# Three layers of an image network: waits of each tile's own place, a bias on ScalarE, and another order of seven products

## The chip, the core and the metric

The kernel runs on one core of a Trainium2 chip. The metric is device time in microseconds (us) of one execution, taken as the median over several runs. One further execution was recorded by the profiler. Engines are named as in the profile: PE (TensorE, matmuls), DVE (VectorE), ACT (ScalarE), POOL (GpSimd), SP (the queue that issues most transfers). "P1" to "P7" are the seven products of Strassen's method.

## The reference

The input x has two images of 512 channels and 32 x 32 positions, in float32. Four layers follow each other; the output of one is the input of the next.

```python
# layer 0: deformable attention with a learned position bias, then an MLP
attn = softmax(q @ k + cpb_mlp(positions));  x = x + out_w @ (attn @ v) + out_b
x = x + mlp_w2 @ gelu(mlp_w1 @ bn2(x) + mlp_b1) + mlp_b2
# layer 1: linear attention
Q, K, V = wq @ x + bq, wk @ x + bk, wv @ x + bv
Q, K = Q / norm(Q), K / norm(K)                       # over the 64 channels
tailor = 1 / (n + Q^T @ (K.sum(-1) + eps))
x = x + gamma * (V.sum(-1) + Q^T @ (K @ V^T)) * tailor
# layers 2 and 3: group norm, attention with 8 heads of 64, projection, residual
qkv = qkv_w @ group_norm(x) + qkv_b
a = softmax(q^T @ k * scale) @ v                      # per head
x = x + proj_w @ a + proj_b
```

## The kernel before

x stays in SBUF for the whole kernel: `self.xs[b][t]`, for image b and a block t of 128 channels, 1024 positions wide. The class `Net` has one method per stage. In time they follow each other: layer 0 with its position bias and attention (to about 2045 us), its MLP `mlp0` (2046 to 2431), `layer1` (2431 to 2500), and `attention` twice, for k = 2 (2500 to 2943) and k = 3 (2943 to the end).

Every tile comes from a pool that a stage opens and closes (`Net.pool`, L68). A pool opened later lies on bytes that closed pools left. By default a tile in such a pool waits until every user of all those pools has finished. The framework can also make it wait only for the users of the bytes under this very tile (for PSUM, of its bank).

Where a block stands under `manual_schedule`, the engines named there execute in the order of the program text. Elsewhere a scheduler orders the instructions of an engine.

**MLP.** `mlp0` runs eight slabs of two times seven products (`m_0P` to `m_7P`, L729). Weights are prepared by left sums (L707 to L710) on POOL.

**Layer 1.** `l1qk` (L894) makes queries and keys of both images. `l1t` (L909) transposes x, block by block of positions; even blocks are copied to SBUF by ACT (L913), odd ones by DVE (L915). POOL squares, DVE reduces, ACT takes the root, DVE divides. Then the written order begins: `keys_sum` (kb), `divisors`, `keys_x` (m1), `keys_column`, `turned` (transposed queries, qt), `matrix` (m and the tile mat), `result` (w, L1002). For image 0 DVE adds w to x; for image 1 ACT copies it to ws (L1011) and POOL adds (L1012). Between them stand the statistics and the first normalized block of layer 2 (`channel_means`, `group_means`, `norm_first`: L1283 to L1324). The PSUM pools are ps_t (three buffers, transposes), ps_m and ps (three buffers, everything else).

**Heads (k = 2, 3).** `queries_keys_values` makes q, k and v with seven products each (qk20P and so on, L1152), with left sums of the weights on POOL. `heads_bounded` then goes through 16 units, each an image b, a pair p of heads, and a half h of the queries (512 positions). A unit has eight steps n. In the written order, `score` of a step (L1366, then the exponential L1370 on ACT) stands two steps ahead of its `value` (L1395). The exponentials are summed on POOL (`some`, L1375, L1377) and on DVE (`sum`, L1380 to L1384). Four steps into the next unit comes `divide`: matmuls sum over partitions (d, L1412), ACT copies one half, DVE adds the other, takes the reciprocal (L1418), multiplies (L1420) and adds the bias of v (L1421). The scheduler places ACT's work; PE, DVE and POOL keep the written order.

In the second half of the units, `sums` for the projection are spread over POOL, three per unit and later two (L1431, and left sums). The last subtracts, `late`, run on DVE after the last divide.

PSUM places have names, and `place(spot, name)` gives the next tile in one: "a", "b", "even", "odd".

**Projection.** `project(b)` makes seven products for image b. Each has two halves of the output, and DVE, ACT or POOL adds each half to those blocks of x that need it. `add(eng, p, i, what)` adds to block i of half p, from PSUM or from a tile; u (and u3) are sums over products that several blocks share. `store(p, i)` in layer 3 writes a finished block to memory from SP. Before, the products come in this order, with the sums u and u3 in SBUF:

```python
for which, spot in zip(("P1", "P3", "P2", "P6", "P7", "P5", "P4"), at):
```

With k = 2 the second projection also carries the start of layer 3's normalization: `channel_means(3, 0, t)` for four channel blocks, `group_means` (matmul gm3, L1290, then dv, L1293 to L1295, and a second matmul L1297, sc and off L1298 to L1310), and `norm_first` (xn300, L1324).

Of the kernel before, what the change touches and what calls it, by code (L numbers as in the profile page):

```python
# [11 lines left out]
F32 = mybir.dt.float32  # L12
# [6 lines left out]
P = 128  # L19
# [35 lines left out]
class Net:  # L55
# [808 lines left out]
    def layer1(self, w, bias):  # L864
# [3 lines left out]
        with ExitStack() as ctx:  # L868
            pool = self.pool(ctx, "l1")
            small = self.pool(ctx, "l1s", 3)  # L870
            last = self.pool(ctx, "l1w", 4)
            ps_t = self.pool(ctx, "l1_ps_t", 3, psum=True)
            ps_m = self.pool(ctx, "l1_ps_m", 1, psum=True)
# [11 lines left out]
            for b in range(B):  # L885
                qk.append(pool.tile([P, NB, 2, DH], F32, tag=f"qk{b}", name=f"qk{b}"))
                xT.append(pool.tile([P, NB, C], F32, tag=f"xT{b}", name=f"xT{b}"))
                for half in range(2):
                    qk_ps = ps.tile([P, 4, P], F32, tag="ps", name=f"l1qk{b}{half}")
                    for i in range(4):  # L890
                        n = 4 * half + i
                        for t in range(CT):
                            xt = self.xs[b][t][:, n * P : (n + 1) * P]
                            nc.tensor.matmul(  # L894
                                qk_ps[:, i, :], lhsT=xt, rhs=w[:, t, C:640], start=(t == 0), stop=(t == CT - 1)
                            )
                    nc.vector.tensor_tensor(
                        qk[b][:, 4 * half : 4 * half + 4, :, :].rearrange("p n a d -> p n (a d)"),
                        qk_ps,
                        bias[:, C:640].unsqueeze(1).to_broadcast([P, 4, P]),  # L900
                        ALU.add,
                    )
            for b in range(B):
                sq = pool.tile([P, NB, 2, DH], F32, tag=f"sq{b}", name=f"sq{b}")
                nc.gpsimd.tensor_tensor(sq, qk[b], qk[b], ALU.mult)
                for n in range(NB):
                    tr = ps_t.tile([P, C], F32, tag="t", name=f"l1t{b}{n}")
                    for t in range(CT):
                        nc.tensor.transpose(  # L909
                            tr[:, t * P : (t + 1) * P], self.xs[b][t][:, n * P : (n + 1) * P], self.ident  # L910
                        )
                    if n % 2 == 0:
                        nc.scalar.copy(xT[b][:, n, :], tr)  # L913
                    else:
                        nc.vector.tensor_copy(xT[b][:, n, :], tr)  # L915
# [66 lines left out]

            def turned(b):
                for h in range(2):
                    tr = ps_t.tile([P, HF], F32, tag="t", name=f"qt{b}{h}")
                    for n in range(4):
                        nc.tensor.transpose(tr[:, n * P : (n + 1) * P], qn[b][:, 4 * h + n, :], self.ident)
                    qa = pool.tile([DH + 1, HF], F32, tag=f"qa{b}{h}", name=f"qa{b}{h}")
                    act.copy(qa, tr[0 : DH + 1, :])
                    q_at.append(qa)  # L990

            def matrix(b):
# [24 lines left out]
            with self.tc.manual_schedule(engines=engines):  # L1017
# [5 lines left out]
                keys_column(0)  # L1023
                turned(0)
                matrix(0)
                keys_sum(1)

# [246 lines left out]

    def channel_means(self, k, b, t):
        nc, small = self.nc, self.norm
        if t == 0:
# [54 lines left out]
    def heads_bounded(self, k, ones, data, proj, out):  # L1332
# [7 lines left out]
        with ExitStack() as ctx:  # L1340
# [66 lines left out]
            def divide(unit):  # L1407
# [12 lines left out]
                nc.vector.tensor_tensor(res, res, t, ALU.mult)  # L1420
                nc.vector.tensor_scalar(res, res, self.col(f"vb{k}", p), None, ALU.add)  # L1421

# [4 lines left out]
            left = [proj[:, i] for i in range(4)] + [more[:, i] for i in range(3)]  # L1427
            right, sums, late = [], [], []

            def subtract(eng, to, x, y):  # L1430
                return lambda: eng.tensor_tensor(to, x, y, ALU.subtract)  # L1431

            for b in range(B):
# [8 lines left out]
                if b == 1:  # L1442
                    sums += self.left_steps(nc.gpsimd, proj, more)
                    sums += [subtract(nc.gpsimd, t1[c], r[1][c], r[0][c]) for c in range(2)]
                for c in range(2):
                    eng, to = (nc.vector, late) if b == c == 1 else (nc.gpsimd, sums)
                    if b == 0:
                        to.append(subtract(eng, t1[c], r[1][c], r[0][c]))
                    to.append(subtract(eng, t2[c], r[3][c], t1[c]))
                    to.append(subtract(eng, t3[c], r[3][c], r[1][c]))  # L1450
                    to.append(subtract(eng, t4[c], r[2][c], t2[c]))

            def project(b):
# [10 lines left out]
                def store(p, i):  # L1464
                    o = 2 * (i // 2) + p
                    cut = slice((i % 2) * HF, (i % 2 + 1) * HF)
                    if out is not None:
                        nc.sync.dma_start(out[b, o][:, cut], self.xs[b][o][:, cut])

                at = ("a", "b", "even", "a", "b", "even", "a") if b == 0 else ("odd", "even", "b", "odd", "even", "a", "b")  # L1470
                for which, spot in zip(("P1", "P3", "P2", "P6", "P7", "P5", "P4"), at):
                    a, ri = SEVEN[which]
                    if which == "P1":
                        us = ap2.tile([P, 2, HF], F32, tag="sum", name=f"pu{k}{b}")
                    elif which == "P7":
                        u3s = ap2.tile([P, 2, HF], F32, tag="sum", name=f"pv{k}{b}")
                    acc = place(spot, f"pb{k}{b}{which}")
# [289 lines left out]
```

## Time and profile before

| | us |
|---|---|
| median of three runs | 3387.63 (3387.11 to 3388.1) |
| the profiled execution | 3386.91 |
| its span, first to last instruction | 3385.1 |
| last matmul ends, from the span's start | 3377.07 |
| mean granted clock of TensorE | 0.999 |

Times in the text are microseconds from the span's start in the profiled execution. A group's line shows line, engine, operation, output and inputs with their shapes and the number of instructions; then its busy time, the mean of one in nanoseconds, and the idle time of the engine just ahead of them with what ended most of it. A waits line shows the waiting group, what it waited for, the total, how often, and the longest. A timeline line shows start, duration, engine, line, operation and tiles, and in square brackets the idle time ahead of it.

Busy time in microseconds by stage, in the same profile:

| stretch | PE | DVE | ACT | POOL |
|---|---|---|---|---|
| 2431 to 2500, layer 1 | 64.75 | 36.87 | 14.57 | 20.51 |
| 2627 to 2886, heads of layer 2 | 254.79 | 209.09 | 152.23 | 149.97 |
| 2886 to 2942, projection of layer 2 | 52.15 | 42.02 | 5.82 | 17.40 |
| 3070 to 3326, heads of layer 3 | 252.96 | 206.23 | 149.20 | 148.06 |
| 3326 to 3385, projection of layer 3 and end | 51.06 | 36.80 | 3.70 | 19.10 |

### The profile page before, as it was taken

To read this page: it belongs to the slowest core of one execution; us is meant where nothing else is said; L and a number is where in the kernel's file an instruction comes from. 1 tells how busy PE (TensorE), PEld (TensorE's weight loads), DVE (VectorE), ACT (ScalarE), POOL (GpSimd) and SP (SyncE) were. 2 spreads that over 40 slices of the span, in tenths; PEclk is the share of its full clock that TensorE was granted. 3 is DMA by queue.
4 is the path that set the end of the run, shared out by engine and by line. 5 is a ranking of instruction groups with operands and counts; after the bars stand their busy time and mean duration, and the time that the engine had idled before them with its cause. 6 is when DMAs were issued, how large, how long until landed. Compare 5 with 4: busy or idle time off the path is not lost.

```text
span 3385.1 us, 60157 instructions
## 1 busy us (share of the span) xinstructions
PE 3335.1 (99%) x25224; PEld 1241.3 (37%) x25224; DVE 2377.3 (70%) x2544; ACT 2040.8 (60%) x2152; POOL 2169.6 (64%) x1643
## 2 busy tenths in 40 slices
PE   7999999999999999999999999999999999999999
PEld 2333333333333333333333334444555433355433
DVE  6777777777766677777766664575466689765897
ACT  6887887887886688887887761111121566213662
POOL 4877877878877677878878873432324357444474
PEclk9999999999999999999999999999999999999999
DMA  6877877877877577877787861111000100000001
GB/s 164 160 148 156 159 156 149 165 155 156 161 155 144 118 158 147 165 155 156 161 171 159 161 158 64 50 37 38 0 1 2 37 2 1 14 0 13 1 1 51
DMA packets 102384, 342.66 MB, mean 101 GB/s; under 512 B 12624, under 2 KB 14288, under 8 KB 99024
## 3 DMA queue, kind: packets, MB, share of 16 engines
q0 software_dynamic: 73296, 266.90, 40.4%
q1 hardware_dynamic: 27792, 69.68, 7.2%
q8 instruction: 203, 3.33, 0.4%
q10 hardware_dynamic: 1008, 2.06, 0.2%
q14 instruction: 85, 0.70, 0.1%
HBM read 67.27 MB, written 4.46 MB: 21 GB/s over the span
## 4 chain that ended last, share of the span: by engine, by line
PE 90%; DVE 6%; POOL 2%; ACT 1%; issue 1%; DMA 0%; ACTq 0%; DVEq 0%; POOLq 0%
PE hp L559 51%; PE s L1366 4%; PE o L1395 4%; PE sim L591 3%; PE qk20P L1152 1%; PE qk30P L1152 1%; PE m_0P L729 1%; PE m_6P L729 1%; PE m_4P L729 1%; PE m_2P L729 1%; PE m_1P L729 1%; PE qk31P L1152 1%; PE qk21P L1152 1%; PE m_5P L729 1%; PE m_3P L729 1%; PE m_7P L729 1%
## 5 line engine op out<-in xcount | busy, mean ns | idle before, releaser
L559 PE MATMUL hp<-h,w 128*32 128x512 f32 x16384 | 1799.3, 593 | 3.0 <-DVE h L528 2.0
L528 DVE CUSTOM_DVE_ANT_1 h<-tx,bank 128x1024 f32<-128x1024 f32 x1024 | 1180.8, 1216 | 308.6 <-PE hp L559 236.8
L564 ACT ACTIVATE h<-hp,magb 128x1024 f32<-128x1024 f32 x1024 | 1120.7, 1111 | 378.0 <-PE hp L559 370.2
L559 PEld LDWEIGHTS hp<-h,w 128*32 128x32 f32 x16384 | 527.8, 110 | 1204.3 <-issue 1148.3
L551 POOL DMA_DIRECT2D h<-h x509 | 451.6, 1022 | 385.2 <-ACT h L570 323.3
L577 POOL TENSOR_TENSOR h<-h,h 128x1024 f32<-128x1024 f32 x255 | 610.0, 2392 | 21.3
L575 POOL TENSOR_SCALAR h<-h,flip 128x1024 f32<-128x1024 f32 x256 | 447.0, 1746 | 0.9 <-ACT h L564 0.9
L1370 ACT ACTIVATE e<-s 128x1024 f32<-128x1024 f32 x256 | 261.7, 1024 | 159.8 <-PE s L1366 159.1
L566 ACT ACTIVATE h<-h,flip 128x1024 f32<-128x1024 f32 x256 | 291.4, 1138 | 0.0
L1395 PE MATMUL o<-e,v 64*64 64x512 f32 x2048 | 267.7, 589 | 0.8 <-ACT e L1370 0.8
L1366 PE MATMUL s<-q,k 64*64 64x512 f32 x2048 | 267.9, 589 | 0.0
L1375 POOL TENSOR_TENSOR some<-e,e 128x1024 f32<-128x1024 f32 x32 | 75.5, 2360 | 172.6 <-DVE sum L1384 139.2
L1377 POOL TENSOR_TENSOR some<-some,e 128x1024 f32<-128x1024 f32 x64 | 167.0, 2609 | 23.7 <-ACT e L1370 20.1
L568 POOL TENSOR_SCALAR h<-h,flip 128x1024 f32<-128x1024 f32 x128 | 143.0, 1117 | 51.6 <-ACT h L564 50.7
L570 ACT ACTIVATE h<-h,flip 128x1024 f32<-128x1024 f32 x128 | 145.6, 1138 | 0.0
L591 PE MATMUL sim<-h,ends 128*32 128x512 f32 x1024 | 135.3, 592 | 0.1
L1395 PEld LDWEIGHTS o<-e,v 64*64 64x64 f32 x2048 | 83.3, 133 | 137.4 <-issue 132.0
L1366 PEld LDWEIGHTS s<-q,k 64*64 64x64 f32 x2048 | 83.2, 133 | 136.1 <-issue 123.5
L707 POOL TENSOR_TENSOR mlp_w<-mlp_w 128x512 f32<-128x512 f32 x16 | 22.4, 1401 | 160.1 <-DMA mlp_w<-in_mlp_w 124.3
L1380 DVE TENSOR_TENSOR sum<-e,e 128x1024 f32<-128x1024 f32 x32 | 81.0, 2531 | 62.5 <-ACT e L1370 62.5
L788 ACT ACTIVATE mh<-mh,cols 128x512 f32<-128x512 f32 x64 | 46.2, 722 | 124.3 <-DVE mh L806 65.2
L1418 DVE RECIPROCAL r<-r 128x512 f32<-128x512 f32 x32 | 107.3, 3353 | 1.1
(537 smaller groups left out, 3308.0 us busy)
## 6 DMA issues: line engine op xcount, KB each, us to landing
h<-h POOLq DMA_DIRECT2D x509, 512.0 KB, 6.4
lb<-logs SPq DMA_DIRECT2D x63, 512.0 KB, 5.2
mlp_w<-in_mlp_w SPq DMA_DIRECT2D x16, 1024.0 KB, 4.9
x<-in_x SPq DMA_DIRECT2D x8, 512.0 KB, 9.4
qkw<-in_l_qk SPq DMA_DIRECT2D x2, 2048.0 KB, 7.5
out<-x SPq DMA_DIRECT2D x16, 256.0 KB, 2.5
vw<-in_l_v SPq DMA_DIRECT2D x2, 1024.0 KB, 7.6
projw<-in_l_proj SPq DMA_DIRECT2D x2, 1024.0 KB, 4.7
```

The costliest lines, as they stand in the source:

```text
L528: self.nc.vector._custom_dve(TENSOR_ADD_SAT, out=h[:, k, :, :], in0=x[:, jj, 2 * r + k, :].unsqueeze(1).to_broadcast([P, H, W]), in1=y[:, ...
L551: nc.gpsimd.dma_start(to, what, accum_op=ALU.add)
L559: nc.tensor.matmul(hp[rows, cut], lhsT=self.l0w2[:, 32 * q : 32 * q + 32], rhs=h1[k][:, cut], start=True, stop=True)
L564: nc.scalar.activation(y, hp, AF.Relu, bias=self.magb[:, q : q + 1])
L566: nc.scalar.activation(ys[0], ys[0], AF.Copy, scale=self.flip[:, 0:1])
L575: nc.gpsimd.tensor_scalar(y, y, self.flip[:, 2:3], 1.0, ALU.mult, ALU.mult)
L577: (nc.vector if final else nc.gpsimd).tensor_tensor(y, y, ys[2], ALU.add)
L591: nc.tensor.matmul(sims[u][at : at + 32, :], lhsT=self.ends[:, 28 - 4 * o : 60 - 4 * o], rhs=z[jj][:, h * HF : (h + 1) * HF], start=(o == ...
L729: self.nc.tensor.matmul(acc[p], lhsT=w[:, a, k, p * P : (p + 1) * P], rhs=right(r, k), start=k == 0, stop=k == 1)
L1366: nc.tensor.matmul(s[halves[c], par, :], lhsT=ks[p][rows, at : at + DH], rhs=qs[p][rows, cut], start=True, stop=True)
L1370: nc.scalar.activation(e, s, AF.Exp, scale=DH**-0.5)
L1395: nc.tensor.matmul(o[halves[par], r, :], lhsT=v[n // 2][rows, n % 2, at : at + DH], rhs=e[rows, par, :], start=(n == 0), stop=(n == NB - 1),)
```

## The change

Five things are changed. No matmul is added or taken away.

1. Every pool is opened so that a tile waits only for what was in its own place.
2. In `layer1` the transposes and `l1qk` share two PSUM pools of three buffers each (ps and the new ps_q); `turned` handles one half at a time, the second after `matrix`; mat is made in two halves.
3. In `heads_bounded` the bias after the divide goes from DVE to ACT (all units but the last), four steps after the divide and ahead of that step's values; ACT's order is written out too; the `late` subtracts go from DVE to POOL; POOL makes two sums per unit throughout and the rest after the last unit.
4. `project` takes the products in another order. P5 and P7 go from PSUM straight to two blocks each by DVE, u goes to three blocks by POOL after P6, and u3 is gone.
5. With k = 2 the statistics for layer 3 are spread over the first three products, and its group means stand after P5 and P3, one product later than before.

```diff
-        return ctx.enter_context(self.tc.tile_pool(name=name, bufs=bufs, **kind))
+        return ctx.enter_context(self.tc.tile_pool(name=name, bufs=bufs, reuse_waits="tile", **kind))
...
-            ps_t = self.pool(ctx, "l1_ps_t", 3, psum=True)
+            ps_q = self.pool(ctx, "l1_ps_q", 3, psum=True)
...
-                    qk_ps = ps.tile([P, 4, P], F32, tag="ps", name=f"l1qk{b}{half}")
+                    qk_ps = ps_q.tile([P, 4, P], F32, tag="ps", name=f"l1qk{b}{half}")
...
-                    tr = ps_t.tile([P, C], F32, tag="t", name=f"l1t{b}{n}")
+                    tr = (ps, ps_q)[n % 2].tile([P, C], F32, tag="ps", name=f"l1t{b}{n}")
...
-            def turned(b):
-                for h in range(2):
-                    tr = ps_t.tile([P, HF], F32, tag="t", name=f"qt{b}{h}")
...
+            def turned(b, h):
+                tr = ps_q.tile([P, HF], F32, tag="ps", name=f"qt{b}{h}")
...
-                vec.scalar_tensor_tensor(mat, bias[0 : DH + 1, 0:C], kss[b], m_ps, ALU.mult, ALU.add)
+                for cut in (slice(0, C // 2), slice(C // 2, C)):
+                    vec.scalar_tensor_tensor(
+                        mat[:, cut], bias[0 : DH + 1, cut], kss[b], m_ps[:, cut], ALU.mult, ALU.add
+                    )
...
-                turned(1)
+                turned(1, 0)
                 matrix(1)
+                turned(1, 1)
...
-                nc.vector.tensor_scalar(res, res, self.col(f"vb{k}", p), None, ALU.add)
+                if unit is units[-1]:
+                    nc.vector.tensor_scalar(res, res, self.col(f"vb{k}", p), None, ALU.add)
+                else:
+                    biases.append(lambda: nc.scalar.activation(res, res, AF.Identity, bias=self.col(f"vb{k}", p)))
...
-                    eng, to = (nc.vector, late) if b == c == 1 else (nc.gpsimd, sums)
+                    to = late if b == c == 1 else sums
...
-                for which, spot in zip(("P1", "P3", "P2", "P6", "P7", "P5", "P4"), at):
+                for which, spot in zip(("P1", "P2", "P6", "P5", "P3", "P7", "P4"), at):
...
-                        elif which == "P3":
-                            add(vec, p, 1, got, True)
...
+                        elif which == "P5":
+                            add(vec, p, 1, got)
+                            add(vec, p, 3, got)
+                        elif which == "P3":
+                            add(vec, p, 1, got, True)
+                            store(p, 1)
                         elif which == "P7":
-                            u3 = u3s[:, p, :]
-                            vec.tensor_tensor(u3, got, u, ALU.add)
-                            add(pool, p, 3, u3)
-                            if p == 1:
-                                for q in range(2):
-                                    add(pool, q, 2, u3s[:, q, :])
-                        elif which == "P5":
-                            vec.tensor_tensor(u, got, u, ALU.add)
-                            add(pool, p, 1, u)
-                            store(p, 1)
                             add(vec, p, 3, got, True)
                             store(p, 3)
+                            add(vec, p, 2, got)
...
+                    if which == "P6":
+                        for i in (1, 3, 2):
+                            for p in range(2):
+                                add(pool, p, i, us[:, p, :])
...
-            engines = {getattr(mybir.EngineType, e) for e in ("PE", "DVE", "Pool")}
+            engines = {getattr(mybir.EngineType, e) for e in ("PE", "Activation", "DVE", "Pool")}
...
+                    if i % NB == 0 and biases:
+                        biases.pop(0)()
                     if i >= 2:
                         value(*steps[i - 2])
...
-                        for _ in range(3 if i < len(steps) * 3 // 4 else 2):
+                        for _ in range(2):
                             sums.pop(0)()
-                assert not sums
+                for do in sums:
+                    do()
...
-                        if n < 2:
-                            self.channel_means(3, 0, 2 * n)
-                            self.channel_means(3, 0, 2 * n + 1)
-                        elif n == 2:
+                        if n < 3:
+                            for t in ((0, 1), (2,), (3,))[n]:
+                                self.channel_means(3, 0, t)
+                        elif n == 3:
...
-                        elif n == 3:
+                        elif n == 4:
                             next(means, None)
                             self.norm_first(3)
```

More of the change, by code (lines that the diff above doesn't have):

```diff
@@ L981, in divisors @@
                 )
-            def turned(b):
-                for h in range(2):
-                    tr = ps_t.tile([P, HF], F32, tag="t", name=f"qt{b}{h}")
[L986 to L990, printed above, removed]
+            def turned(b, h):
+                tr = ps_q.tile([P, HF], F32, tag="ps", name=f"qt{b}{h}")
+                for n in range(4):
+                    nc.tensor.transpose(tr[:, n * P : (n + 1) * P], qn[b][:, 4 * h + n, :], self.ident)
+                qa = pool.tile([DH + 1, HF], F32, tag=f"qa{b}{h}", name=f"qa{b}{h}")
+                act.copy(qa, tr[0 : DH + 1, :])
+                q_at.append(qa)
             def matrix(b):
@@ L1023, in layer1 @@
                 keys_column(0)
-                turned(0)
+                turned(0, 0)
                 matrix(0)
+                turned(0, 1)
                 keys_sum(1)
@@ L1420, in divide, with subtract @@
                 nc.vector.tensor_tensor(res, res, t, ALU.mult)
-                nc.vector.tensor_scalar(res, res, self.col(f"vb{k}", p), None, ALU.add)
+                if unit is units[-1]:
+                    nc.vector.tensor_scalar(res, res, self.col(f"vb{k}", p), None, ALU.add)
+                else:
+                    biases.append(lambda: nc.scalar.activation(res, res, AF.Identity, bias=self.col(f"vb{k}", p)))
             more = wp.tile([P, 3, 2, 2 * P], F32, tag="proj", name=f"projm{k}")
             left = [proj[:, i] for i in range(4)] + [more[:, i] for i in range(3)]
-            right, sums, late = [], [], []
-            def subtract(eng, to, x, y):
-                return lambda: eng.tensor_tensor(to, x, y, ALU.subtract)
+            right, sums, late, biases = [], [], [], []
+            def subtract(to, x, y):
+                return lambda: nc.gpsimd.tensor_tensor(to, x, y, ALU.subtract)
             for b in range(B):
@@ L1443, in heads_bounded @@
                     sums += self.left_steps(nc.gpsimd, proj, more)
-                    sums += [subtract(nc.gpsimd, t1[c], r[1][c], r[0][c]) for c in range(2)]
+                    sums += [subtract(t1[c], r[1][c], r[0][c]) for c in range(2)]
                 for c in range(2):
-                    eng, to = (nc.vector, late) if b == c == 1 else (nc.gpsimd, sums)
+                    to = late if b == c == 1 else sums
                     if b == 0:
[L1448 to L1451, printed above, removed]
+                        to.append(subtract(t1[c], r[1][c], r[0][c]))
+                    to.append(subtract(t2[c], r[3][c], t1[c]))
+                    to.append(subtract(t3[c], r[3][c], r[1][c]))
+                    to.append(subtract(t4[c], r[2][c], t2[c]))
             def project(b):
@@ L1468, in store @@
                         nc.sync.dma_start(out[b, o][:, cut], self.xs[b][o][:, cut])
+                us = ap2.tile([P, 2, HF], F32, tag="sum", name=f"pu{k}{b}")
                 at = ("a", "b", "even", "a", "b", "even", "a") if b == 0 else ("odd", "even", "b", "odd", "even", "a", "b")
-                for which, spot in zip(("P1", "P3", "P2", "P6", "P7", "P5", "P4"), at):
+                for which, spot in zip(("P1", "P2", "P6", "P5", "P3", "P7", "P4"), at):
                     a, ri = SEVEN[which]
[L1473 to L1476, printed above, removed]
                     acc = place(spot, f"pb{k}{b}{which}")
```

## The prediction, as made before the change was run

> **What bounds the kernel now.** I read the page's busy shares and its chain first, then TensorE's waits, then the groups of one stretch of the heads, then single stretches in time.
>
> ```profile
> PE 3335.1 (99%) x25224; PEld 1241.3 (37%) x25224; DVE 2377.3 (70%) x2544; ACT 2040.8 (60%) x2152; POOL 2169.6 (64%) x1643
> PE 90%; DVE 6%; POOL 2%; ACT 1%; issue 1%; DMA 0%; ACTq 0%; DVEq 0%; POOLq 0%
> ```
>
> TensorE (PE) is busy 99% and is 90% of the chain that ended last. The change alters no matmul, so all it can win is PE's idle time, what an idle stretch does to PE's clock, and the 8.0 us between PE's last matmul (3377.07) and the span's end. The waits of PE list that idle time:
>
> ```profile
> PE d L1412 <- DVE q L1405: 6.2, 8, 1.5
> PE gm L1290 <- DVE mv L1284: 3.0, 1, 3.0
> PE qk30P L1152 <- DVE x L1460: 1.8, 1, 1.8
> PE l1t L909 <- DVE xT L915: 1.6, 2, 0.8
> PE qk20P L1152 <- ACT ws L1011: 1.3, 1, 1.3
> PE l1qk L894 <- DVE x L824: 0.9, 1, 0.9
> PE m_0P L729 <- POOL mlp_w L709: 0.9, 1, 0.9
> PE w L1002 <- DVE gm L1291: 0.8, 1, 0.8
> PE o L1395 <- ACT e L1370: 0.8, 1, 0.8
> ```
>
> The columns are total us, times, longest. The rest of PE's waits lies in layer 0 and its start, where the order of instructions is the same after the change. These nine rows hold 17.3 us. Each of them is taken up below.
>
> **Heads.** The row "d" is the divide (L1412), whose matmuls wait until DVE has run through its queue. These are DVE's groups between 2815 and 2881 us, in the second half of layer 2's heads:
>
> ```profile
> L1382 DVE TENSOR_TENSOR sum<-sum,e 128x1024 f32<-128x1024 f32 x9 | 16.9, 1881 | 0.5
> L1380 DVE TENSOR_TENSOR sum<-e,e 128x1024 f32<-128x1024 f32 x5 | 14.8, 2967 | 0.3 <-ACT e L1370 0.2
> L1418 DVE RECIPROCAL r<-r 128x512 f32<-128x512 f32 x4 | 13.4, 3353 | 0.1
> L1384 DVE TENSOR_TENSOR sum<-sum,some 128x1024 f32<-128x1024 f32 x5 | 6.1, 1225 | 0.5
> L1421 DVE TENSOR_SCALAR q<-q,cols 128x512 f32<-128x512 f32 x4 | 5.5, 1387 | 0.1
> L1420 DVE TENSOR_TENSOR q<-q,r 128x512 f32<-128x512 f32 x4 | 4.8, 1208 | 0.1
> L1405 DVE TENSOR_TENSOR q<-o,q 128x512 f32<-128x512 f32 x5 | 3.4, 684 | 0.0
> L1417 DVE TENSOR_TENSOR r<-d,r 128x512 f32<-128x512 f32 x4 | 2.7, 678 | 0.0
> ```
>
> A unit of eight steps costs DVE 2.97 + 2 x 1.88 + 3.35 + 1.23 + 1.39 + 1.21 + 0.68 + 0.68 = 15.3 us, with next to no idle time. PE's own unit is 14.82: from the end of one divide gap to the start of the next, 2833.18 to 2848.0. DVE is therefore the bound in these four units of each layer, by 0.3 us where POOL makes two sums per unit and by 1.2 to 1.5 where it makes three. The change moves the bias (L1421, 1.39) to ACT and makes it two sums everywhere: 15.3 - 1.4 = 13.9, under 14.82. I take all 6.2 us. ACT has room: eight exponentials of 1.02 and two copies of 0.58 are 9.4 of 14.82, and a bias is near the 0.81 of L1322, which has the same operation and shape. What is late next is that bias, which waits for DVE's multiply (L1420) with an exponential behind it. Counting from the divide's start, the multiply ends at 8.2 and so does the exponential ahead of the bias, so it waits 0.1 at most, and the score places give PE about 1.2 us before it feels a late exponential.
>
> **Table.** The row "o" is an ACT table load of 1.28 us at 2648.89 in front of layer 2's first exponential. Now that ACT's order is written out, the early Sqrt stays behind the heads and the load goes: **-0.8**.
>
> **Waits by place.** m_0P waited for every user of layer 0's pools; now its own first bank was long free: **-0.9**. l1qk (0.9) also starts earlier, but in front of the end of kb0 stands a chain that doesn't move: POOL's sums until 2441.25, its square to 2443.10, then DVE's reduction and the copies of xT. With six buffers in place of three the two l1t stalls go, but the transposes with a DVE copy still share three buffers and stall around 2450. By that walk the first m1 matmul stays at 2457.0: **0**, between -0.9 (all of l1qk kept) and +0.3. In the second half m1 starts 0.5 earlier, the matrix comes in halves, and the first xn of layer 2 (DVE, ends 2499.77) releases qk20P in place of the last ws copy (2500.08): rows "w" and "qk20P" hold 2.1, I take **-1.0**, between -0.5 and -2.1.
>
> **Projection.** P5's place is freed by four DVE adds instead of two and two. With the late subtracts and five sums on POOL beside them, P4 of the first batch may wait 0.2 to 0.6 in each layer: **+0.4**, from 0 to 1.2. The late subtracts cost PE nothing: they are issued after the third product, about T+10 on the scale below, and the first product that reads them (P6 of the second batch) starts near T+32.
>
> **From layer 2 to 3.** This is the term I know least. Before, gm3 waits 2.97 us, and PE's clock falls behind that gap: 0.87 in 2922-2926 and 0.70 in 2926-2930, against 1.00 around them. The eight matmuls of the product behind it take 5.0 us from start to start instead of 3.44 (the starts 2911.60, 2915.03, 2918.47), so 1.5 more. The gaps of 1.77 and 1.48 leave the clock at 1.00. [...]
>
> In the new order gm3 stands one product later and its gap shrinks to about 0.9. But P6's u now goes to POOL as six adds of 1.24, and layer 3's left sums (2.42 each) follow at once; before they began at 2942.53. They meet DVE's small steps of the normalization. What that does shows at 2495, under the adds of layer 1, with 0.16 as the price alone (L1309 at 2932.68):
>
> ```profile
> 2493.32 7.57 POOL L1012 TENSOR_TENSOR x<-x,ws 128x512 f32<-128x512 f32 x6 [43.21 <-ACT ws L1011]
> 2495.31 0.52 DVE L1301 TENSOR_TENSOR sc<-sc,cols 128x4 f32<-128x4 f32 x1
> 2495.87 1.19 DVE L1309 TENSOR_TENSOR off<-gm,sc 128x4 f32<-128x4 f32 x1
> 2497.09 1.19 DVE L1310 TENSOR_TENSOR off<-cols,off 128x4 f32<-128x4 f32 x1
> 2498.32 1.45 DVE L1324 TENSOR_SCALAR xn<-x,sc,off 128x512 f32<-128x512 f32 x1
> ```
>
> Each DVE step ends with a POOL operation. The reciprocal among them (0.18) and the evictions from PSUM do not. [...]
>
> I walk it from the start of the first projection, T = 2886.24; layer 3's first matmul was at T+56.65. POOL's adds stand at about T+38 to T+45.4, the left sums to T+55.4. The last of P5's adds on DVE needs POOL's fourth and ends at T+43.6. Then come three steps of dv, and after a matmul and the root L1301, L1309, L1310 and xn300, with six evictions (4.3) behind them, of which the last releases qk30P. Without a clash that is T+53.55: **-3.1**. With one step per POOL operation xn300 ends at T+55.9 and qk30P starts at T+60.3: **+3.7**, and the clock may fall once more (+1.5). Between left sums POOL pauses 0.08 us (2944.95 to 2945.03), and DVE needs 0.04 to its next step, so two steps may slip through each border: T+55.75, **-0.9**. The rows show one step per operation, but under adds without such a pause. I take the middle of the last two, **+1.4**.
>
> **Tail.** Before, the last stores queue on SP behind POOL's add that ends 3378.45, and the last is issued at 3380.15 and lands at 3384.16. Now the last follows P4's second eviction, 1.5 after PE: **-1.5**, from -1 to -2.
>
> **Sum.** -6.2 - 0.8 - 0.9 + 0 - 1.0 + 0.4 + 1.4 - 1.5 = -8.6. The profiled execution took 3386.91 for its span of 3385.1, which goes to 3376.5. It is 0.7 under the median 3387.63, so I predict 3379.0. A measurement of this kernel can tell about 0.2%, 6.8 us, from no change: faster means under 3380.85.
>
> **The rivals.**
> - **A free transition.** If the left sums do no harm, +1.4 becomes -3.1: -13.1, 3374.5; with l1qk's 0.9 kept, 3373.6. For it speaks that before only DVE's xn waited under left sums. Against it stand the four rows above.
> - [...] +3.7 in place of +1.4 gives -6.3, 3381.3; with the clock's 1.5, 3382.8. That is inside 0.2%. Four rows speak for it, the pause of 0.08 against it.
> - **Slower: ACT's queue.** The bias is the one new wait in ACT's order, thirty times over two layers, with an exponential and so PE's values behind it. It costs PE what it is late over 1.2 us. At 1.8 us late it costs 0.6 x 30 = 18 us: -8.6 + 18 = +9.4, 3397. It decides from 0.29 over the 1.2 (8.6 / 30), and is slower beyond 0.2% from 0.51. For it: three DVE operations stand between divide and multiply, and all contended rows are long. Against: DVE has 0.9 spare per unit, and ACT 4.6.
> - **Nothing is gained.** If other waits stand behind those removed, the divide above all, the 6.2 stays and the sum is -2.4, 3385.2, within 0.2%.
>
> **How the numbers follow.** Forecast 0.44; free transition 0.22; lock at full price 0.22; ACT's queue 0.06; nothing gained 0.06. The full price lies near the border, and a quarter of it (0.06) I count as faster. Faster: 0.44 + 0.22 + 0.06 = 0.72; same 0.16 + 0.06 = 0.22; slower 0.06. The range reaches from the free case with l1qk kept, 3373.6, to the full price with its second clock loss (3382.8) and the dear ends of projection and tail (+0.8, +0.5): 3384.1. It leaves out ACT's queue, half of the nothing-gained case, and some of both ends.
>
> **What would show it.** Right: the rows "d", "o" and "m_0P" gone from PE's waits; ACT's idle time in front of the bias near zero; the last store issued about 1.5 after PE's last matmul; layer 3's first matmul near T+58. Full price: L1301 to L1324 each over 2 us after P3 of layer 2's second batch. Wrong: scores or values waiting for ACT in the heads, new PE waits in layer 1 above 0.9 us, or P4 waiting more than 1.2.

## The result, and the profile after

| | before | after |
|---|---|---|
| median of 16 runs each | 3387.82 (3386.72 to 3392.71) | 3380.59 (3379.94 to 3383.1) |
| span of the profiled execution | 3385.1 | 3378.4 |
| last matmul ends | 3377.07 | 3373.89 |

The ratio is 0.9978, with a 95% interval of 0.9971 to 0.9986. The change gains 7.2 us where 8.6 were forecast; 3380.59 stands against the predicted 3379.0. The page after, busy shares and chain:

```profile
PE 3332.5 (99%) x25224; PEld 1230.0 (36%) x25224; DVE 2341.7 (69%) x2518; ACT 2057.7 (61%) x2180; POOL 2181.1 (65%) x1649
PE 94%; DVE 2%; POOL 2%; issue 1%; ACT 1%; DMA 1%; ACTq 0%; POOLq 0%; DVEq 0%
```

PE's share of the chain rose from 90% to 94%. The waits of PE after:

```profile
PE bank L618 <- DVE ss L614: 6.0, 1, 6.0
...
PE qk30P L1158 <- DVE x L1470: 2.8, 1, 2.8
...
PE l1t L911 <- DVE xT L917: 1.9, 1, 1.9
PE gm L1304 <- DVE dv L1302: 1.7, 1, 1.7
PE bank L635 <- DVE e L631: 1.5, 1, 1.5
PE qk20P L1158 <- DVE xn L1331: 1.1, 1, 1.1
PE l1t L911 <- DVE qk L899: 1.0, 1, 1.0
PE pb21P L1487 <- DVE sc L1305: 1.0, 1, 1.0
...
PE gm L1297 <- DVE mv L1291: 0.6, 1, 0.6
```

The rows "d", "o", "l1qk", "m_0P" and "w" are gone. At the top stands a row that the prediction did not have: 6.0 us in layer 0, whose code is untouched. From the starts of PE's groups in both traces, each stage's change, in us:

| stage | forecast | measured |
|---|---|---|
| start to the last products of layer 0 (2012.8) | 0 | +0.13 |
| from there to m_0P | -0.9 | +7.75 |
| MLP, first half of layer 1 | 0 | -0.16 |
| second half of layer 1 | -1.0 | -0.92 |
| layer 2 to its first divide (table load) | -0.8 | -1.15 |
| heads of layer 2 | -3.3 | -4.79 |
| heads of layer 3 | -2.9 | -4.43 |
| first batch of both projections | +0.4 | +0.26 |
| layer 2 to 3 | +1.4 | +0.14 |
| after the last matmul | -1.5 | -3.58 |
| sum | -8.6 | -6.75 |

**Layer 0.** The end of layer 0 in the timeline, before:

```profile
2016.35 2.83 DVE L763 TENSOR_SCALAR mx<-x,bn2s,cols 128x512 f32<-128x512 f32 x6
2019.21 1.23 DVE L715 TENSOR_TENSOR mx<-mx,mx 128x1024 f32<-128x1024 f32 x1
2024.27 1.96 POOL L707 TENSOR_TENSOR mlp_w<-mlp_w 128x512 f32<-128x512 f32 x1 [11.17 <-DMA mlp_w<-in_mlp_w]
```

and after:

```profile
2016.68 8.53 DVE L763 TENSOR_SCALAR mx<-x,bn2s,cols 128x512 f32<-128x512 f32 x6
2025.25 2.17 DVE L715 TENSOR_TENSOR mx<-mx,mx 128x1024 f32<-128x1024 f32 x1
2027.34 0.74 DVE L614 TENSOR_SCALAR ss<-sim,cols 128x512 f32<-128x512 f32 x1
2016.28 1.62 POOL L707 TENSOR_TENSOR mlp_w<-mlp_w 128x512 f32<-128x512 f32 x1 [2.84 <-DMA mlp_w<-in_mlp_w]
2017.97 1.34 POOL L708 TENSOR_TENSOR mlp_w<-mlp_w 128x512 f32<-128x512 f32 x1
```

The MLP's first weights no longer wait for whole pools, so their transfer lands and POOL's left sums begin 8 us earlier. There they meet six of the eight mx steps on DVE, which then take 8.53 instead of 2.83. Those stand in DVE's queue ahead of ss (L614), which the last softmax of layer 0 waits for. ss comes 7.0 later, at 2027.34 instead of 2020.35.

PE stands still 6.0 for it, and pays once more behind it. The windows view shows the length of a stretch, the busy time and count of PE, PEld, DVE, ACT and POOL, then PE's granted clock, the DMA share and GB/s:

```profile
2024.74:2028.16 3.42, 0.03 (x1) 0.03 (x1) 3.39 (x4) 0.00 (x0) 3.26 (x3) 0.50 0.35 146
2028.16:2031.57 3.41, 3.41 (x7) 1.89 (x8) 3.41 (x2) 0.00 (x0) 3.33 (x3) 0.50 0.00 0
```

PE works at half clock from its restart at 2028.13 to 2031.57, which costs about 1.7. Before, the clock was 1.00 there. The parts add up: 6.0 for ss, 0.9 more for e, the softmax's result (1.49 for 0.59), 1.7 for the clock, less the 0.9 of m_0P, make 7.7 of the 7.75.

**Layer 2 to 3.** DVE and POOL after:

```profile
2931.26 1.18 DVE L1301 TENSOR_TENSOR dv<-dv 128x4 f32<-128x4 f32 x1
2934.52 0.43 DVE L1308 TENSOR_TENSOR sc<-sc,cols 128x4 f32<-128x4 f32 x1
2934.98 0.16 DVE L1316 TENSOR_TENSOR off<-gm,sc 128x4 f32<-128x4 f32 x1
2935.18 2.20 DVE L1317 TENSOR_TENSOR off<-cols,off 128x4 f32<-128x4 f32 x1
2937.41 2.72 DVE L1331 TENSOR_SCALAR xn<-x,sc,off 128x512 f32<-128x512 f32 x1
2932.50 2.42 POOL L707 TENSOR_TENSOR qkm<-qkw 128x1024 f32<-128x1024 f32 x1
2935.00 2.35 POOL L708 TENSOR_TENSOR qkw<-qkw 128x1024 f32<-128x1024 f32 x1
2937.43 2.42 POOL L709 TENSOR_TENSOR qkm<-qkw 128x1024 f32<-128x1024 f32 x1
```

L1308 ends with the first left sum (2934.92), L1316 begins in the pause of 0.08 behind it, and L1317 and xn each take as long as a whole sum. Layer 3's first matmul starts 56.9 after the first projection, against 56.65 before.

### The profile page after: what moved, and what is told of

It is laid out like the page before. It is cut to its first block, busy times and chain, and to the rows that moved or that the text cites. A ratio compares the mean times of both kernels' runs of the same rounds, so it can differ in the third digit from the quotient of the medians.

```text
span 3378.4 us, 60140 instructions
## 1 busy us (share of the span) xinstructions
PE 3332.5 (99%) x25224; PEld 1230.0 (36%) x25224; DVE 2341.7 (69%) x2518; ACT 2057.7 (61%) x2180; POOL 2181.1 (65%) x1649
## 4 chain that ended last, share of the span: by engine, by line
PE 94%; DVE 2%; POOL 2%; issue 1%; ACT 1%; DMA 1%; ACTq 0%; POOLq 0%; DVEq 0%
PE hp L559 51%; PE s L1373 7%; PE o L1402 7%; PE sim L591 3%; PE qk30P L1158 1%; PE qk20P L1158 1%; PE m_0P L729 1%; PE m_6P L729 1%; PE m_5P L729 1%; PE m_3P L729 1%; PE qk31P L1158 1%; PE qk21P L1158 1%; PE m_4P L729 1%; PE m_2P L729 1%; PE m_1P L729 1%; PE m_7P L729 1%
## 5 line engine op out<-in xcount | busy, mean ns | idle before, releaser
L1387 DVE TENSOR_TENSOR sum<-e,e 128x1024 f32<-128x1024 f32 x32 | 57.1, 1784 | 100.2 <-ACT e L1377 100.2
```

## The experiments

All times are medians, with the lowest and highest run, beside the change's 3380.59. The kernel before ran again beside each of them, with medians of 3387.81 to 3388.08.

**1. The MLP's weights as before.** A new branch in `Net.pool` shifts later line numbers by two.

```diff
-        return ctx.enter_context(self.tc.tile_pool(name=name, bufs=bufs, reuse_waits="tile", **kind))
+        if name not in ('m_w',):
+            kind["reuse_waits"] = "tile"
+        return ctx.enter_context(self.tc.tile_pool(name=name, bufs=bufs, **kind))
```

> The changed kernel, but the pool of the MLP's weights (m_w) waits for whole pools again. Theory (POOL's first left sums start at 2016 instead of 2024 and meet DVE's eight mx steps, L763, which stand in front of ss, L614): the sums start near 2024 again, L763 takes 0.55 instead of 1.50, the wait of PE for ss (6.0) and that for e (1.5) shrink by 6.9, and with the 0.9 of m_0P kept the first MLP product starts near 2045.1: 3380.6 - 8.7 = 3372, between 3371 and 3373.5. Rival (the wait for ss comes from something else that the new waits set free, such as transfers or another order on DVE): the wait of 6.0 stays and the time is 3380.6, within 1.

Measured 3373.32 (3372.89 to 3373.87), ratio to before 0.9956 (0.9942 to 0.9969). Its timeline:

```profile
2016.18 2.82 DVE L765 TENSOR_SCALAR mx<-x,bn2s,cols 128x512 f32<-128x512 f32 x6
2024.16 1.90 POOL L709 TENSOR_TENSOR mlp_w<-mlp_w 128x512 f32<-128x512 f32 x1 [11.23 <-DMA mlp_w<-in_mlp_w]
```

The sums are late again, the six steps short, PE's wait for ss is gone and that for e is 0.7. The MLP starts at 2044.7 instead of 2053.8; from the last products of layer 0 to there it takes 8.7 less, the theory's figure. One pool's wait was worth 7.3 us to the whole. The difference to 8.7 lies mostly in a clock loss of 1.7 in layer 1 (last section).

**2. The mx steps on ACT, the sums still early.**

```diff
-                        vec.tensor_scalar(
-                            r[i][:, k, :],
...
+                        if b == 0:
+                            nc.scalar.activation(
+                                r[i][:, k, :], x, AF.Identity, scale=s2[:, t : t + 1], bias=self.col("bn2_b", t)
+                            )
+                        else:
+                            vec.tensor_scalar(r[i][:, k, :], x, s2[:, t : t + 1], self.col("bn2_b", t), ALU.mult, ALU.add)
```

> The changed kernel, but the eight mx steps (L763) of image 0 run on ACT (0.8 each, by the row of L1322) and the left sums start early as in the change. Theory (DVE and POOL keep each other out): with the eight steps off DVE only the first right sum (L715) stands in front of ss, which comes about 2 late instead of 7: 3380.6 - 5 = 3375.6, between 3373 and 3378. Rival (the early start of POOL or its transfers cost by themselves, whatever DVE does): 3380.6, within 1.5.

Measured 3377.94 (3377.43 to 3378.53), 0.9969 (0.9957 to 0.9982). The timeline of ACT and DVE:

```profile
2013.36 5.76 ACT L765 ACTIVATE mx<-x,cols,bn2s 128x512 f32<-128x512 f32 x8 [1.15 <-DVE bn2s L96]
2019.15 2.13 DVE L715 TENSOR_TENSOR mx<-mx,mx 128x1024 f32<-128x1024 f32 x1 [3.34 <-ACT mx L765]
2021.21 0.74 DVE L614 TENSOR_SCALAR ss<-sim,cols 128x512 f32<-128x512 f32 x1
```

With the same early sums, ACT's steps take 0.72 each, ss starts 0.9 after its time of before, not 7.0, and PE does not wait for it. From the last products of layer 0 to the MLP it takes 4.3 less than in the change, half of the 8.7 of experiment 1. The right sums on DVE still pay: L715 to L718 take 7.7 instead of 4.9. The softmax's steps between them keep their times and come later, so PE waits 3.2 for e (0.6 before), and behind that wait the clock halves for 3.41. The early transfer itself costs nothing to be seen: in the change two mx steps stand beside it (2013.49 and 2015.09; DMA share 0.91 in 2012 to 2014 and 0.69 in 2014 to 2016) and take 0.55 and 0.54, as before, where the share is 0.00. The gain of 2.7 lies under the 5 of the forecast, since those later steps were left out of it, and a clock loss in layer 1 came on top.

**3. Old waits everywhere: parts 2 to 5 alone.**

```diff
-        return ctx.enter_context(self.tc.tile_pool(name=name, bufs=bufs, reuse_waits="tile", **kind))
+        return ctx.enter_context(self.tc.tile_pool(name=name, bufs=bufs, **kind))
```

> The changed kernel with the old waits of whole pools everywhere: parts 2 to 5 alone. Theory (part 1 is a loss in layer 0 and otherwise worth little): m_0P starts near 2046, as before; layer 1 is as in the change but qk20P waits for the last ws copy, +0.3; layer 3's left sums begin after the last x add, so that the steps L1308 to L1331 are short and qk30P starts 0 to 3 us earlier from the projection's start: 3380.6 - 7.9 + 0.3 - 1.5 = 3371.5, between 3370 and 3374. Rival (the parts need each other, and the old waits bring back stalls at stage borders): over 3376.

Measured 3373.67 (3373.2 to 3376.31), 0.9958 (0.9945 to 0.9972): 14.1 under before. The total is as the theory had it, one step of it is not: layer 3's left sums begin as early as in the change (2925.05, right behind POOL's last add, 45.4 after the projection's start in both). With the new waits and the old order of products (experiment 8) they begin at 57.8. Their early start comes from the new order, not from the new waits.

**4. New waits alone, on the kernel before.** The same line, the other way round.

> The kernel before with the waits of each tile's place, part 1 alone. Theory: POOL's early sums cost 8.6 at the end of layer 0, m_0P gains 0.9, qk20P 0.3, and the rest stays: 3387.8 + 7.4 = 3395, between 3393 and 3397. Rival (shorter waits only ever help): 3385 to 3387.8.

Measured 3394.33 (3393.54 to 3398.82), 1.002 (1.0011 to 1.0029). Part 1 by itself makes the kernel slower by 6.5; the wait for ss (6.0) is in its trace too.

**5. New waits but for the MLP's weights, on the kernel before.** The edit of experiment 1.

> The kernel before with the waits of each tile's place, but for the MLP's weight pool. Theory (the whole loss of part 1 is the early left sums): the MLP starts 0.9 earlier than before, layer 2 about 0.2 to 1.2 earlier, the rest stays: 3387.6 - 0.8, between 3386 and 3388. Rival (other early starts collide too): 3389 and over.

Measured 3386.89 (3384.79 to 3387.86), 0.9995 (0.9986 to 1.0004). The loss is gone, so it sat in that pool. Whether the other new waits gain is not settled by it: the interval holds no change. In its trace layer 2 starts 0.9 earlier than before, and right there the clock halves (2499.26 to 2502.68) and takes 1.6 back.

**6. The bias back on DVE.**

```diff
-                if unit is units[-1]:
-                    nc.vector.tensor_scalar(res, res, self.col(f"vb{k}", p), None, ALU.add)
-                else:
-                    biases.append(lambda: nc.scalar.activation(res, res, AF.Identity, bias=self.col(f"vb{k}", p)))
+                nc.vector.tensor_scalar(res, res, self.col(f"vb{k}", p), None, ALU.add)
```

> The changed kernel with every bias back on DVE; POOL keeps two sums per unit. Theory (the bias on DVE makes DVE the bound of the late units): DVE needs 15.3 a unit and PE 14.59, as in the units of before that made two sums, which took 15.12 to 15.14. Six or seven units in each layer lose 0.53: 3380.6 + 6.4 = 3387.0, between 3385.5 and 3388.5. Rival (the third sum on POOL was what made the units late, and the bias fits): 3380.6 to 3382.

Measured 3385.73 (3384.85 to 3387.2), 0.9991 (0.9982 to 1.0). In each layer four units, not seven, took 14.94 to 15.14 instead of 14.59: 2.0 a layer. The rest of the 5.1 lies mostly in layer 2 to 3, where the clock halved behind the same gaps that left it full in the change (last section).

**7. Three sums per unit again.**

```diff
-                        for _ in range(2):
-                            sums.pop(0)()
+                        for _ in range(3 if i < len(steps) * 3 // 4 else 2):
+                            if sums:
+                                sums.pop(0)()
```

> The changed kernel with the old spread of POOL's sums in the heads: three per unit where before had three; the bias stays on ACT. Theory (DVE's total per unit is the bound, so the move of the bias pays in these units too): DVE needs 16.0 to 16.3 less 1.4, or 14.6 to 14.9, against PE's 14.59, in two or three units of each layer: 3380.6 plus 0.5 to 1.5. With this run and the one with the bias on DVE the heads' gain of 9.2 splits. Rival (the third sum is the larger part by itself): 3383 and over.

Measured 3386.39 (3386.14 to 3388.93), 0.9997 (0.9988 to 1.0006). The rival is right: the third sum costs 3.1 a layer though the bias is on ACT. A wait of PE, and the bias on ACT's timeline that makes it:

```profile
PE s L1373 <- ACT e L1377: 3.7, 2, 1.8
```

```profile
2877.24 0.72 ACT L1431 ACTIVATE q<-q,cols 128x512 f32<-128x512 f32 x1 [3.31 <-POOL v L1441]
```

The bias waits 3.3 for a POOL sum (L1441, ends 2877.20) and holds back the exponential behind it, and PE waits 1.8 for a score's place. It is the prediction's slower rival with another cause: not the multiply was late, but POOL. In the change itself the biases wait 1.3 in all in layer 2, and PE not at all. Moving the bias and spreading the sums need each other: without the first the heads lose 4.0 of their 9.2, without the second 6.1.

**8. The old order of products.** `project` and layer 3's statistics as in the kernel before, all else as in the change.

```diff
-                for which, spot in zip(("P1", "P2", "P6", "P5", "P3", "P7", "P4"), at):
+                for which, spot in zip(("P1", "P3", "P2", "P6", "P7", "P5", "P4"), at):
```

> The changed kernel with the old order of products, old sums u and u3, and layer 3's statistics where they were. Theory (the new order pays at the end, and in the transition its shorter gm3 wait is eaten by the DVE steps that meet POOL): the time from the last matmul to the end goes from 4.5 back to 8.1, the transition from 56.9 to about 56.6 after the projection's start: 3380.6 + 3.6 - 0.3 - 0.2 = 3383.7, between 3382.5 and 3385. Rival (the new order wins in the transition too): over 3385. Rival (the new order costs more in the transition than it wins at the end): under 3380.

Measured 3383.88 (3381.1 to 3384.76), 0.9984 (0.9975 to 0.9993). From the last matmul to the end it takes 7.9 instead of 4.5, about the 3.3 by which the medians differ. The new order pays at the end. The transition was expected at 56.6 and takes 58.0 in this trace: behind gm's wait of 3.0 the clock halves for 6.83, where it halved for 3.41 in the kernel before.

**9. dv through PSUM.**

```diff
...
+        if k == 3 and b == 0:
+            d0 = ps[:, 0, 2 * CT : 3 * CT]
+            nc.vector.tensor_tensor(d0, mv[:, :, 0], ps[:, 0, 0:CT], ALU.subtract)
+            nc.vector.tensor_tensor(dv, mv[:, :, 0], ps[:, 0, 0:CT], ALU.subtract)
+            nc.vector.tensor_tensor(d0, d0, dv, ALU.mult)
+            nc.vector.tensor_tensor(dv, d0, mv[:, :, 1], ALU.add)
...
```

> The changed kernel; in layer 3's group means each of the small dv steps has one input in PSUM instead of two in SBUF, with one step more. Theory (a DVE step waits for POOL because both its inputs come from SBUF): the steps take about 0.16 each instead of 0.42 and 1.18, PE's second gm matmul comes 1.2 earlier and its wait of 1.7 nearly goes; what is late next is sc (1.0), also 1 earlier. qk30P waits behind xn, L1331, under a left sum, as before: 3380.6 less 0 to 1.3. Rival (any DVE step behind a POOL operation waits): the steps stay at 1.2, and the time at 3380.6 to 3381.

Measured 3382.76 (3380.84 to 3385.8), 0.9983 (0.9974 to 0.9992). DVE's timeline, a multiply of dv with one input in PSUM, and later steps with both in SBUF:

```profile
2933.42 0.17 DVE L1304 TENSOR_TENSOR gm<-gm,dv 128x4 f32<-128x4 f32 x1
...
2935.66 1.62 DVE L1315 TENSOR_TENSOR sc<-sc,cols 128x4 f32<-128x4 f32 x1
...
2937.51 2.20 DVE L1324 TENSOR_TENSOR off<-cols,off 128x4 f32<-128x4 f32 x1
2939.75 2.71 DVE L1338 TENSOR_SCALAR xn<-x,sc,off 128x512 f32<-128x512 f32 x1
```

The first step of the theory is shown: beside POOL's adds, the multiply takes 0.17 instead of 1.18 and the two subtracts ahead of it 0.16 each, and gm's wait falls from 1.7 to 0.5. The time is not better. The 1.2 won are spent at L1315, which now meets the first left sum near its start and takes 1.62 instead of 0.43; qk30P waits 4.0, and the transition takes 56.9 as in the change. The profiled execution is one of the longest of these eleven runs (3385.11): the clock halves for 3.41 at 2507.50 and for 6.83 from 2944.41, within that wait of 4.0, which together costs 4.0. Three runs lie at 3380.8 to 3381.0.

**10. Layer 3's left sums on DVE.**

```diff
-            def left_side(i):
+            def left_side(i, eng=nc.gpsimd):
...
-                self.left_sums(nc.gpsimd, w, more)
+                self.left_sums(eng, w, more)
...
-            left_side(0)
+            if k == 2:
+                left_side(0)
...
                 vec.tensor_tensor(dqk, self.colr(f"qb{k}", CT), self.colr(f"kb{k}", CT), ALU.subtract)
+                if k == 3:
+                    left_side(0, vec)
```

> The changed kernel with layer 3's left sums of the query and key weights on DVE, behind its normalized blocks, so that none runs on POOL while L1308 to L1331 do. Theory: L1317 takes 0.16 instead of 2.20 and xn (L1331) 0.55 instead of 2.72, the evictions behind them follow PE, and qk30P's wait of 2.8 falls to about 1.5: 3380.6 - 1.3 = 3379.3, between 3378.5 and 3380.2. Rival (the left sums on DVE come too late for P3, or delay the evictions of layer 3): 3381 and over.

Measured 3382.24 (3378.7 to 3383.22), 0.9978 (0.9969 to 0.9987). DVE's steps in its profiled execution, and layer 3's first matmul 55.6 after the projection's start instead of 56.9:

```profile
2935.27 0.17 DVE L1320 TENSOR_TENSOR off<-cols,off 128x4 f32<-128x4 f32 x1
2935.47 0.55 DVE L1334 TENSOR_SCALAR xn<-x,sc,off 128x512 f32<-128x512 f32 x1
```

The trace gives the 1.3 of the theory, and qk30P's wait is 1.5. That wait alone would not show it: it is 1.5 in experiment 1 too, where POOL still makes the sums and PE comes late from a clock loss, and there the transition takes 57.3. The median does not give the 1.3: five runs lie between 3378.7 and 3380.2 with a mean clock of 0.999, six between 3382.2 and 3383.2 with 0.998. Five lie where the theory put them. The six above have the lower mean clock, so a clock loss is the likely reason; the trace is of one of the five. By the number the rival (3381 and over) has it, but its mechanism is not in the trace: behind layer 3's first matmul every stage takes as long as in the change.

**11 and 12. Together.** Experiments 1, 9 and 10 in one kernel, and 9 and 10 with the old waits everywhere.

> The changed kernel with three edits together: the MLP's weight pool waits for whole pools, layer 3's left sums of the query and key weights on DVE, dv through PSUM. Theory: 3373.3 for the first alone; qk30P's wait is already down to 1.5 there, PE's waits at gm (1.7) and pb21P (1.0) lose up to 1.2 each but the evictions that end the stage move less: 3372, between 3370.5 and 3373.3. Rival (the transition is bound elsewhere): 3373.3 to 3374.

> Parts 2 to 5 of the change with the old waits of whole pools, layer 3's left sums on DVE and dv through PSUM. Theory: 3373.7 for the old waits alone, less 1 to 2.5 in the transition: 3372, between 3370.5 and 3373. Against the run with the new waits it shows what these are worth once POOL's early sums are out of the way: 0 to 1.

Measured 3370.49 (3370.24 to 3370.75), 0.9949 (0.9935 to 0.9962), and 3370.72 (3370.11 to 3373.15), 0.9951 (0.9937 to 0.9964). Both lie at the low end of what was expected, and beat the kernel before by 17 and the change by 10. The transition takes 54.4 and 54.6, 2.3 to 2.5 less than in the change: with the left sums away, the gain of experiment 9 arrives. The two differ only in the waits and not in time, though the first starts layer 2 1.7 earlier (2497.79 and 2499.45). What becomes of that is told in the last section.

## Why the prediction was right and where it was wrong

The sum was near by luck: at the end of layer 0 a loss of 7.75 stood where a gain of 0.9 was forecast, and the other stages together gained 6.8 more than forecast. Errors of 8.65 and 6.8 all but cancelled.

**The step that failed** is "The rest of PE's waits lies in layer 0 and its start, where the order of instructions is the same after the change." The order is the same; the times are not. A wait that part 1 shortened, of a transfer, let POOL start 8 us earlier beside DVE. Such a collision was in the prediction, shown at 2495 (1.19 for 0.16) and priced for layer 2 to 3, and only there. Experiments 1, 4 and 5 show that the loss of part 1 hangs on this one pool, and experiment 2 that half of it goes when the mx steps alone leave DVE; the other half is read from the stretched right sums and the clock in its trace. A price of the clock behind a gap was in the prediction too, 1.5 behind the gap of 2.97; here it was 1.7 and not counted.

**Heads**: right in kind, too small in size. The term was 6.2, the sum of PE's idle time; the units of before lost 9.2. PE's unit is 14.59, as the undisturbed units of both traces show, and the late ones took 16.30, 16.01, 15.12, 15.14 and so on. The 14.82 was taken from the end of one gap to the start of the next, where the restart is inside. Idle time counts what PE stands still, not what a stop costs.

**Layer 2 to 3**: the forecast lay between one and two steps at each border. The trace shows two at the first (L1308 and L1316) and one at the second (L1317), and 56.9, between the 55.75 walked for two and the 58.05 taken. The clock did not fall behind the gap of 2.80.

**End**: -1.5 came from the issue of the last store alone. That is right as far as it goes (issued 3.1 after the last matmul before, 1.5 now), but the store also landed 2.0 after its issue instead of 4.0. Before, six stores were issued within 3 us and the last of them landed at 3384.16; now two are issued behind the last matmul. Experiment 8, which brings the six queued stores back, has 3.9 again. That the queueing made the difference is read from the traces and was not tried apart from the order of products.

**Waits by place and table**: m_0P's own wait went, and layer 1 gave back what l1qk won, as forecast; layer 1's second half and the table load came within 0.4. One of the prediction's signs of being wrong did appear, new waits of PE in layer 1 above 0.9: l1t waits 1.9 and 1.0 (0.8 twice before). They are the stalls that its walk put around 2450, and the first m1 matmul came out 0.16 earlier, counted from the MLP's start, where 0 was forecast.

**The rivals**: the free transition and the full price, a whole POOL operation for each DVE step (+3.7), did not occur; ACT's queue did not in the change, and did in experiment 7; the waits named in "nothing is gained" went, and no others took their place in the heads.

## What to carry to other kernels

When waits are loosened, list for every engine what starts earlier, transfers included, and look what stands beside it then; an unchanged order proves nothing. A helper's early work is worth something only if its result is late, and POOL's first four sums, which ended at 2030.6 before, had 15 us to spare to the MLP's start, while DVE's queue had none. Price a stall by the spacing of whole units with and without it, not by the idle column.

## What the runs showed of the hardware

Whether a DVE step was held up beside POOL went by where its operands lay, not by its size alone. A multiply of 128x4 with both inputs in SBUF took 1.18 beside a POOL add of 1.26, and 0.17 with one input in PSUM (experiment 9); ss, 128x512 read from PSUM, took 0.74 beside a left sum as without one. Steps of 128x512 with one input from SBUF (mx) paid as well, 1.42 for 0.47 on average of six. Why these did is not shown.

The clock's losses depend on more than the gap. After the first 33 us the traces have two values of the granted clock, 1.00 and 0.50, and the halved stretches told of here that end within the kernel last 3.41 us (before, from 2924.98) or 6.83 us (the change, from 2024.74). In one trace the changes lie on a grid of 3.413: in the change the clock rises at 2031.57 and halves at 3376.42, behind the last matmul, 394 steps apart; before, it rises at 2928.39 and halves at 3382.37, 133 steps apart; in experiment 1 it halves at 2463.81 and at 2928.03, 136 steps apart. Where the grid lies differs from trace to trace (43.0 and 42.2, below). In experiment 1 the loss of layer 1 stands between two edges of it:

```profile
2460.40:2463.81 3.41, 3.41 (x40) 3.41 (x40) 0.00 (x0) 0.38 (x1) 0.00 (x0) 1.00 0.00 0
2463.81:2467.23 3.42, 3.42 (x9) 1.55 (x8) 0.15 (x1) 0.58 (x1) 0.00 (x0) 0.50 0.00 0
2467.23:2470.64 3.41, 3.41 (x19) 1.95 (x18) 0.87 (x2) 0.69 (x2) 0.00 (x0) 1.00 0.00 0
```

The change does the same matmuls up to there at the same spacing (the first m matmul at 2455.62 and 2464.73, the column sums s 7.14 and 7.15 later) and keeps its full clock:

```profile
2471.89:2475.30 3.41, 3.41 (x27) 2.06 (x27) 0.15 (x1) 0.96 (x2) 0.00 (x0) 1.00 0.00 0
```

In the transition, the same two waits of 1.7 and 1.0 end at 2934.48 and 2935.87 in experiment 6 and at 2932.70 and 2934.09 in the change:

```profile
2934.00:2938.00 4.00, 2.52 (x5) 1.40 (x6) 3.59 (x9) 0.20 (x1) 3.84 (x3) 0.63 0.02 4
2938.00:2942.00 4.00, 4.00 (x6) 1.47 (x6) 3.85 (x2) 0.81 (x1) 3.84 (x3) 0.51 0.02 6
```

```profile
2934.00:2938.00 4.00, 3.91 (x9) 1.82 (x10) 3.59 (x6) 0.80 (x2) 3.84 (x3) 1.00 0.01 4
2938.00:2942.00 4.00, 3.22 (x8) 1.14 (x6) 4.00 (x5) 0.22 (x1) 3.92 (x2) 1.00 0.03 8
```

The first is experiment 6, where the clock halves from 2935.07 to 2941.90; the second is the change, at full clock, where even the gap of 2.80 at 2941 left it at 1.00. A grid step begins 43.0 after the projection's start in experiment 6 and 42.2 in the change. At layer 2's start the clock halves in experiment 11 (first line) and not in 12 (second), nor in experiment 1, which has the instructions and waits of 11 up to there:

```profile
2498.00:2504.00 6.00, 6.00 (x11) 2.50 (x11) 5.93 (x6) 3.57 (x5) 3.59 (x3) 0.72 0.00 0
```

```profile
2498.00:2504.00 6.00, 4.70 (x12) 2.16 (x12) 2.35 (x5) 2.71 (x5) 4.65 (x4) 1.00 0.00 0
```

The values' first product then starts at 2548.08 and 2548.07: the 1.7 that the new waits won are gone. In experiments 1 and 2 layer 1 lost as much: from its first m matmul to its first w it takes 15.8 instead of 14.1, at a clock of 0.84 to 0.88 in part. So the same gap cost the clock in one trace and not in another. That it hangs on where the gap falls on the grid is the author's reading: it fits these pairs, and one kernel falling into two groups of runs 3 us apart (experiment 10), and was not tried by itself. What in a step decides it is not settled: PE is busy 1.49 of 3.41 in the step ahead of experiment 6's loss, 1.70 in the same place in the change, without a loss, and all 3.41, with small products, ahead of the loss in layer 1 of experiment 1. A gain of one or two us can be lost by it, as the 1.7 of experiment 11 was.
